# GpSimd issues two kinds of DMA of layer 0's experts: the loads of slots and the stores of results

## The chip, the cores and the metric

The kernel runs on one core of a Trainium2 chip. A core has five engines that run their own instruction streams and meet only at semaphores: TensorE (PE: matrix products; PEld is its weight load), VectorE (DVE), ScalarE (ACT), GpSimd (POOL) and SyncE (SP). DMAs are issued by an instruction in the stream of SP, ACT or GpSimd, and 16 DMA engines then move the data. An engine takes its instructions in order, so an instruction that waits holds up all that come after it on its engine.

The metric is the device time of one execution in microseconds. Before the change it is 2783.87 us, the median of three runs (2782.39 to 2789.58).

## The reference

The program is two layers on x of 8 x 512 tokens with 256 features, all float32. Layer 0 is what matters here:

```python
x = L0_attn_x
xn = _layernorm(x, axis=-1)
x = x + _L0_attn_ref(xn, ...) + _L0_ffn_ref(xn, L0_ffn_Wg, L0_ffn_W1, L0_ffn_W2, L0_ffn_W3)
xn = _layernorm(x, axis=-1)
x = x + _L1_attn_ref(xn, ...) + _L1_ffn_ref(xn, ...)
```

`_L0_attn_ref` is a linear recurrence in time, run forwards and backwards (16 heads, a state of 16 x 16 per head, a decay that depends on the token), with projections before it and a group norm and a projection after it. `_L0_ffn_ref` is a mixture of eight experts, of which each token takes the two with the highest scores:

```python
scores = xt @ Wg.T
topk_scores, topk_idx = jax.lax.top_k(scores, TOP_K)
gate = jax.nn.silu(jnp.einsum('td,ehd->teh', xt, W1))
up = jnp.einsum('td,ehd->teh', xt, W2)
y = jnp.einsum('teh,edh->ted', gate * up, W3)
out = jnp.einsum('te,ted->td', w, y)
```

Both parts of layer 0 read the same normed x, so they can be computed beside each other. Layer 1 is attention (one global, one local block) and another mixture of experts.

## The kernel before

**Routing and slots.** The kernel first norms and routes all eight sequences (`norm_and_route`, `place`). Each token and each of its two experts gets a slot, a row in the DRAM tensor `slots`; slots of one expert are together, in chunks of 256 rows. There are 39 chunks. `scatter` (L372) writes the tokens to their slots with 64 indirect DMAs on GpSimd.

**The experts.** `experts` (L410) goes through the chunks. For chunk i it has GpSimd gather the weights of the chunk's expert (`weights`, L386: `wgu` for gate and up, 1.4 MB in two buffers; `wdn` for down, 0.75 MB in one). `load_slots` (L394) loads the 256 rows of a chunk from `slots` into `xs` (two buffers), `turned` (L401) transposes them on TensorE, ACT copies the transposed rows to `xT` (L418), and TensorE computes gate and up in three parts (L426), ACT the silu (L452), VectorE the product (L435), and TensorE the down projection `y` (L465). ACT copies `y` to `ys` (L472, one buffer), and a DMA stores `ys` to the DRAM tensor `outs` (L473). The slots of chunk i + 1 are loaded while chunk i is computed, and transposed at the end of the products of chunk i. Layer 1 later gathers the rows of `outs` (L903).

**The recurrence.** `scans` (L674) goes through 128 steps: 8 sequences, 2 halves of the features, 8 pairs of values. A step multiplies a tile `kv` by k (L688), runs two scans forwards (L699) and two backwards (L703), multiplies by r (L708), all on VectorE, and leaves sums over the keys to TensorE (L714), which are issued for two steps at a time. The tile `kv` (four buffers) is filled one step ahead by `spread` (L660): eight DMAs of 64 KB on SP (L665), which read the projection v of that sequence from the DRAM tensor `vd`. `projections` (L480) computes the next sequence's v, k, r, decay and gates while the scans of one sequence run; it loads `xnT` on SP (L485), and GpSimd makes some of its additions (L572). `ending` (L726) norms and projects the result of a sequence (L737 to L785), with a product on GpSimd (L767), a load of x (L730) and a store (L785) on SP.

**What sets the order.** Layer 0 is written as generators. `scans` yields four times a step, and at each yield every running generator (the experts, the projections, the endings) goes on by one turn. The order in which these emit instructions is the order on TensorE, VectorE, ACT and SP: they are pinned by `manual_schedule` (L240, `PINNED` in L35). GpSimd is not pinned; a scheduler puts its instructions in order by its own estimate of when each can run. Waits are inserted automatically, from what each instruction reads and writes. DMAs signal their end on shared semaphores: those that SP and ACT issue take turns on eight of them, in the order of the program, and those that GpSimd issues on eight others; a DMA first waits until the one before it on its semaphore has ended.

Of the kernel before, what the change touches and what calls it, by code (L numbers as in the profile page):

```python
# [165 lines left out]
def two_layers(ctx: ExitStack, tc: tile.TileContext, a: dict, out: bass.AP):  # L166
    nc = tc.nc
    vec_e, act_e, pool_e, pe = nc.vector, nc.scalar, nc.gpsimd, nc.tensor
# [70 lines left out]
    with ExitStack() as l0:  # L239
# [146 lines left out]
        def weights(i, name, of, n, bufs):  # L386
            w = ew.tile([P, n], F32, tag=name, name=f"{name}_{i}", bufs=bufs)
            pool_e.indirect_dma_start(
                out=w, out_offset=None, in_=of,
                in_offset=bass.IndirectOffsetOnAxis(ap=wrow[:, i : i + 1], axis=0),  # L390
            )
            return w

        def load_slots(i):  # L394
            xs = ex.tile([P, NS, D], F32, tag="xs", name=f"xs_{i}", bufs=2)
            nc.sync.dma_start(
                xs, slots[i * CH : (i + 1) * CH].rearrange("(n p) d -> p n d", p=P)
            )
            return xs

        def turned(i, xs):  # L401
            ps = ps_gu.tile([P, NC, CH], F32, tag="gu", name=f"xsT_{i}")
            for c in range(NC):
                for n in range(NS):
                    pe.transpose(
                        ps[:, c, n * P : (n + 1) * P], xs[:, n, c * P : (c + 1) * P], ident
                    )
            return ps

        def experts():  # L410
            nxt = weights(0, "wgu", a["w0_gu"], GU0, 2)
            ps = turned(0, load_slots(0))
            yield
            for i in range(NCH):
                w, xps = nxt, ps
                wd = weights(i, "wdn", a["w0_dn"], DN0, 1)
                xT = ex.tile([P, NC, CH], F32, tag="xT", name=f"xsT_{i}", bufs=1)
                act_e.copy(xT, xps)  # L418
                if i + 1 < NCH:
                    nxt = weights(i + 1, "wgu", a["w0_gu"], GU0, 2)  # L420
                    xs = load_slots(i + 1)
                yield

                def hidden(o, at):
                    for c in range(NC):
                        pe.matmul(  # L426
                            o, w[:, at + c * P : at + (c + 1) * P], xT[:, c, :],
                            start=c == 0, stop=c == NC - 1,
                        )

                hs = [hpool.tile([P, 2, CH], F32, tag="h", name=f"h_{i}_{j}") for j in range(3)]

                def product(j, g, u):
                    n = 2 - j // 2
                    vec_e.tensor_tensor(hs[j][:, :n, :], hs[j][:, :n, :], u[:, :n, :], ALU.mult)  # L435
                    if n == 1:
                        o = hs[j][64:, 1, :]
                        vec_e.tensor_tensor(o, o, g[64:, 1, :], ALU.mult)

                last = None  # L440
                for j in range(3):
                    g = ps_gu.tile([P, 2, CH], F32, tag="gu", name=f"g_{i}_{j}")
                    hidden(g[:, 0, :], 4 * j * D)
                    hidden(g[:, 1, :], (4 * j + 2) * D)
                    yield
                    if last:
                        product(j - 1, *last)
                    u = ps_gu.tile([P, 2, CH], F32, tag="gu", name=f"u_{i}_{j}")
                    n = 2 - j // 2
                    for k in range(n):  # L450
                        hidden(u[:, k, :], (4 * j + 2 * k + 1) * D)
                    act_e.activation(hs[j][:, :n, :], g[:, :n, :], AF.Silu)  # L452
                    if n == 1:
                        act_e.activation(hs[j][64:, 1, :], g[:64, 1, :], AF.Silu)
                    last = g, u
                    yield
                if i + 1 < NCH:
                    ps = turned(i + 1, xs)
                product(2, *last)
                yield  # L460
                y = ps_gu.tile([P, NS, D], F32, tag="gu", name=f"y_{i}")
                for n in range(NS):
                    for j in range(NJ0 + 1):
                        lo = 64 * (j == NJ0)
                        pe.matmul(  # L465
                            y[:, n, :], hs[j // 2][lo:, j % 2, n * P : (n + 1) * P],
                            wd[lo:, j * D : (j + 1) * D], start=j == 0, stop=j == NJ0,
                        )
                        if j % 3 == 2:
                            yield  # L470
                ys = ex.tile([P, NS, D], F32, tag="ys", name=f"ys_{i}", bufs=1)
                act_e.copy(ys, y)  # L472
                act_e.dma_start(  # L473
                    outs[i * CH : (i + 1) * CH].rearrange("(n p) d -> p n d", p=P), ys
                )

# [326 lines left out]
        place()  # L803
        turns.finish()
        turns.add(then(scatter(), experts()))
        for _ in scans(turns):
            turns.turn()
# [616 lines left out]
```

## Time and profile before

| | |
|---|---|
| median of three runs | 2783.87 us |
| profiled execution, device time | 2787.46 us |
| its span, first to last instruction | 2785.7 us |
| PE, PEld busy | 2359.8 us (85%), 1402.9 us (50%) |
| DVE busy | 2137.6 us (77%) |
| ACT busy | 870.1 us (31%) |
| POOL busy | 407.2 us (15%) |
| first slot load, last scan of layer 0 | 237.4 us, 1476.5 us |

The profile is of one execution. Busy time is time in which an engine computes (or, on GpSimd, makes the descriptors of a DMA); instructions that only issue a DMA on SP or ACT are not counted, and stand under SPq and ACTq. "A <- B" in a list of waits means that A stood idle until B ended: total us, times, longest. A wait for several things is put down to the one that ended last, and a DMA's wait is named after the operation that moved the data, such as `kv<-vd`. The chain of waits follows the work that ended last from the end back to the start, at each step to what released it.

### The profile page before, as it was taken

The page shows a single profiled execution, that of the slowest core. Times are in us where ns is not written, and L with a number is a line of the kernel's source. Part 1 is how long each engine was busy: PE and PEld are TensorE (multiplying, and loading weights), DVE is VectorE, ACT ScalarE, POOL GpSimd, SP SyncE. Part 2 cuts the span into 40 slices and gives each one's busy share as a digit, 9 for nine tenths or more (in the row PEclk, how much of TensorE's full clock was granted, in tenths as well). Part 3 has the DMA queues.
Part 4 walks back from the last instruction along what each step waited for, and adds up shares of the span by engine and source line. Part 5 has one row for each costly group of instructions (what it writes and reads, how often), then busy time and mean ns, then how long its engine had stood idle before and what let it go on. Part 6 is the DMA issues. An engine that isn't in the chain of part 4 may idle for free.

```text
span 2785.7 us, 32431 instructions
## 1 busy us (share of the span) xinstructions
PE 2359.8 (85%) x11772; PEld 1402.9 (50%) x11772; DVE 2137.6 (77%) x3042; ACT 870.1 (31%) x1649; POOL 407.2 (15%) x368
## 2 busy tenths in 40 slices
PE   4756888988989889898873899999999989998996
PEld 3313555545555555555651445655555545555554
DVE  4698989899999899889894866667576676667656
ACT  1203231232312323122110234444333434343344
POOL 0074121221212112121102110001010100001000
PEclk8768998999999999999895899999998999999998
DMA  8245454445454444544543100010010100000000
GB/s 281 76 147 168 136 169 130 149 131 168 147 164 136 147 149 145 170 118 149 165 128 140 54 28 24 9 35 28 20 31 31 31 28 27 28 20 28 20 9 16
DMA packets 123886, 263.22 MB, mean 94 GB/s; under 512 B 25264, under 2 KB 76368, under 8 KB 118608
## 3 DMA queue, kind: packets, MB, share of 16 engines
q1 hardware_dynamic: 86912, 129.58, 16.4%
q0 software_dynamic: 17376, 103.69, 11.2%
q10 hardware_dynamic: 19440, 27.87, 2.7%
q8 instruction: 95, 1.56, 0.2%
q14 instruction: 63, 0.52, 0.1%
HBM read 215.17 MB, written 45.88 MB: 94 GB/s over the span
## 4 chain that ended last, share of the span: by engine, by line
PE 49%; DVE 26%; DMA 6%; ACT 4%; issue 3%; SPq 2%; POOL 1%; DVEq 0%; ACTq 0%; POOLq 0%
PE y L1307 6%; PE g L1261 5%; PE u L1261 5%; PE y L465 4%; DVE kv L699 4%; PE g L426 3%; DVE kv L703 3%; DMA kv<-vd 3%; PE sc_g L1159 2%; PE u L426 2%; PE o_g L1187 2%; PE ys L714 2%; SPq L665 2%; DVE kv L688 2%; PE qkv_l L1051 1%
## 5 line engine op out<-in xcount | busy, mean ns | idle before, releaser
L703 DVE TENSOR_TENSOR_SCAN kv<-d,kv 128x512 f32<-128x512 f32 x256 | 336.9, 1316 | 8.8
L699 DVE TENSOR_TENSOR_SCAN kv<-dq,kv 128x512 f32<-128x512 f32 x256 | 320.4, 1252 | 2.5
L426 PE MATMUL g<-xsT,wgu 128*128 128x256 f32 x936 | 249.3, 413 | 32.0 <-ACT xsT L418 31.9
L465 PE MATMUL y<-wdn,h 128*128 128x256 f32 x936 | 259.3, 416 | 11.9 <-DVE h L435 11.9
L1167 ACT ACTIVATE pt_g<-sc_g 128x512 f32<-128x512 f32 (+1 forms) x384 | 171.0, 531 | 237.4 <-PE sc_g L1159 202.8
L426 PEld LDWEIGHTS g<-xsT,wgu 128*128 128x128 f32 x936 | 188.3, 207 | 112.1 <-ACT xsT L418 51.4
L465 PEld LDWEIGHTS y<-wdn,h 128*128 128x128 f32 x936 | 173.8, 200 | 111.1 <-issue 76.7
L1261 PE MATMUL g<-xT,w 128*128 128x512 f32 x384 | 199.6, 645 | 24.4 <-DVE h L1296 9.4
L1261 PE MATMUL u<-xT,w 128*128 128x512 f32 x384 | 190.1, 618 | 18.7 <-DVE h L1296 7.6
L426 PE MATMUL u<-xsT,wgu 128*128 128x256 f32 x780 | 192.8, 387 | 0.0
L714 PE MATMUL ys<-kv,cst 128*32 128x512 f32 x512 | 122.1, 638 | 78.3 <-DVE kv L708 78.1
L688 DVE TENSOR_TENSOR kv<-kv,k 128x1024 f32<-128x1024 f32 x128 | 158.1, 1236 | 37.8 <-DMA kv<-vd 22.0
L1307 PE MATMUL y<-w,h 128*128 128x256 f32 x768 | 179.3, 385 | 0.0
L426 PEld LDWEIGHTS u<-xsT,wgu 128*128 128x128 f32 x780 | 151.6, 196 | 37.9 <-issue 14.8
L708 DVE TENSOR_TENSOR kv<-kv,r 128x1024 f32<-128x1024 f32 x128 | 160.8, 1257 | 3.7
L1279 DVE TENSOR_TENSOR h<-h,u 128x512 f32<-128x512 f32 x96 | 66.0, 688 | 120.5 <-PE u L1261 115.9
L1307 PEld LDWEIGHTS y<-w,h 128*128 128x128 f32 x768 | 141.7, 190 | 32.2 <-issue 9.5
L452 ACT ACTIVATE h<-g 128x512 f32<-128x512 f32 (+1 forms) x117 | 61.6, 526 | 287.8 <-PE g L426 280.2
L1173 DVE TENSOR_TENSOR pt_g<-pt_g,cst 128x512 f32<-128x512 f32 x128 | 85.2, 686 | 69.6 <-ACT pt_g L1167 69.5
L1261 PEld LDWEIGHTS g<-xT,w 128*128 128x128 f32 x384 | 72.5, 202 | 108.3 <-issue 83.9
L1167 ACT ACTIVATE pt_l<-sc_l 128x384 f32<-128x384 f32 (+1 forms) x256 | 98.0, 469 | 90.0 <-PE sc_l L1159 71.9
L1173 DVE TENSOR_TENSOR pt_l<-pt_l,cst 128x768 f32<-128x768 f32 (+1 forms) x128 | 107.9, 885 | 14.8 <-ACT pt_l L1167 14.8
(296 smaller groups left out, 3763.4 us busy)
## 6 DMA issues: line engine op xcount, KB each, us to landing
kv<-vd SPq DMA_DIRECT2D x1024, 64.0 KB, 2.7
cb<-cd SPq DMA_DIRECT2D x128, 128.0 KB, 2.9
slots<-zero SPq DMA_DIRECT2D x1, 9984.0 KB, 35.4
xs<-slots SPq DMA_DIRECT2D x39, 256.0 KB, 4.8
outs<-ys ACTq DMA_DIRECT2D x39, 256.0 KB, 2.1
w<-in_w ACTq DMA_DIRECT2D x12, 384.0 KB, 9.5
xn<-in_x SPq DMA_DIRECT2D x8, 512.0 KB, 8.7
xnT<-xT ACTq DMA_DIRECT2D x16, 256.0 KB, 2.1
```

What stands on the lines that cost most here:

```text
L426: pe.matmul(o, w[:, at + c * P : at + (c + 1) * P], xT[:, c, :], start=c == 0, stop=c == NC - 1,)
L465: pe.matmul(y[:, n, :], hs[j // 2][lo:, j % 2, n * P : (n + 1) * P], wd[lo:, j * D : (j + 1) * D], start=j == 0, stop=j == NJ0,)
L688: vec_e.tensor_tensor(kv, kv, bc(kc, 1, NV), ALU.mult)
L699: vec_e.tensor_tensor_scan(out=kv[:, i, :], data0=qc, data1=kv[:, i, :], initial=0.0, op0=ALU.mult, op1=ALU.add,)
L703: vec_e.tensor_tensor_scan(out=kv[:, i, ::-1], data0=dc[:, ::-1], data1=kv[:, i, ::-1], initial=0.0, op0=ALU.mult, op1=ALU.add,)
L708: vec_e.tensor_tensor(kv, kv, bc(rc, 1, NV), ALU.mult)
L714: pe.matmul(y[r0 : r0 + 32, :], C["take"][:, 24 - 8 * at : 56 - 8 * at], kv[:, i, :], start=at == 0, stop=at == 3, skip_group_check=True,)
L1167: act_e.activation(pt[:, i, :end], scs[i][:, :end], AF.Exp, scale=0.25)
L1173: vec_e.tensor_tensor(pt[:, :, a0 : a0 + m], pt[:, :, a0 : a0 + m], bc(mask[:, :m], 1, 4), ALU.mult,)
L1261: pe.matmul(ps, w[:, k, c * P : (c + 1) * P], xT[:, c, :], start=c == 0, stop=c == NC - 1,)
L1279: vec_e.tensor_tensor(hs[-1], hs[-1], u, ALU.mult)
L1307: pe.matmul(y[:, i, :], hs[k][:, (t + i) * P : (t + i + 1) * P], w1[j - 5 + k][:, 2, :], start=k == 0, stop=k == 5,)
```

## The change

Two DMA issues move to GpSimd's stream: `load_slots` is issued by GpSimd instead of SP (39 loads of 256 KB), and the store of `ys` by GpSimd instead of ACT (39 stores of 256 KB). The data, tiles and buffers stay as they are, and the order of the other instructions on TensorE, VectorE, ACT and SP too. GpSimd's own order is drawn up anew by the scheduler: the 78 DMAs stand among the gathers of weights, the additions of the projections and the products of the endings.

```diff
         def load_slots(i):
             xs = ex.tile([P, NS, D], F32, tag="xs", name=f"xs_{i}", bufs=2)
-            nc.sync.dma_start(
+            pool_e.dma_start(
                 xs, slots[i * CH : (i + 1) * CH].rearrange("(n p) d -> p n d", p=P)
             )
             return xs
...
                 ys = ex.tile([P, NS, D], F32, tag="ys", name=f"ys_{i}", bufs=1)
                 act_e.copy(ys, y)
-                act_e.dma_start(
+                pool_e.dma_start(
                     outs[i * CH : (i + 1) * CH].rearrange("(n p) d -> p n d", p=P), ys
                 )
```

## The prediction

> **What bounds the kernel now.** I read the busy shares first, then one stretch of layer 0, then the waits of VectorE and of SP's DMA queue in it, then the chain there. The change touches only the experts of layer 0, which run from 235 us (the first slots are loaded) to about 1480 us (the last scan). Busy time in that stretch (PE, PEld, DVE, ACT, POOL, each with its count; then TensorE's clock, DMA share, GB/s):
>
> ```profile
> 235.00:1480.00 1245.00, 1067.33 (x4078) 666.48 (x4078) 1129.97 (x1118) 312.07 (x483) 223.65 (x165) 0.93 0.49 147
> ```
>
> VectorE is busy 1130.0 of 1245 us (91%), TensorE 1067.3 (86%), GpSimd 223.7 (18%). So VectorE bounds the stage, with 115 us of idle time in it, and TensorE is close behind. What VectorE waited for (165 to 1500 us: total, times, longest):
>
> ```profile
> DVE kv L688 <- DMA kv<-vd: 22.0, 13, 5.0
> DVE x L782 <- PE o L777: 17.1, 10, 4.4
> DVE kv L688 <- DMA xs<-slots: 15.7, 5, 5.1
> ...
> DVE dx L514 <- DMA xnT<-xnT: 10.9, 2, 6.4
> ```
>
> Line 688 is the first operation of a scan step and needs that step's `kv`; it never reads `xs`. The 15.7 us are the same wait: a slot load stood in SP's queue with the `kv` loads and landed last. So 37.7 us of VectorE's idle time is late `kv`, and 10.9 us a late `xnT`, both loaded by SP. Why is SP late, with loads that could go a step ahead? SP's own waits, 235 to 1480 us:
>
> ```profile
> SPq L665 <- DMA outs<-ys: 389.2, 32, 26.0
> SPq L665 <- PE ys L714: 119.0, 26, 16.2
> SPq L396 <- DMA outs<-ys: 70.6, 7, 14.9
> SPq L665 <- DMA vd<-v: 48.6, 6, 12.1
> ```
>
> 39 waits, 459.8 us, end with the landing of a store of experts' results, which the `kv` load does not need. The instruction order of the built program tells why: the DMAs of SP and ACT share eight completion semaphores in turn, and a DMA first waits for the one that used its semaphore before. Each `outs` store takes a place in that rotation, so within eight DMAs SP stands still until the store has landed; that is after the chunk's product on TensorE and the copy on ACT. The chain of waits has it in full (start, us, what):
>
> ```profile
> 624.80 1.07 PE y L465 x4
> ...
> 625.90 0.59 ACT ys L472
> ...
> 626.51 2.08 DMA outs<-ys
> ...
> 628.62 0.30 SPq L665
> ...
> 628.96 3.50 DMA kv<-vd
> ...
> 632.58 1.24 DVE kv L688
> ```
>
> TensorE finishes `y`, the store takes 2.08 us, SP moves 0.02 us later, `kv` lands 3.50 us after its issue, and VectorE, idle for 2.23 us, starts. I looked at SP and the stores ahead of every VectorE wait over half a microsecond on `kv` (16): fourteen have this form; two (0.58 and 0.73 us) follow a `vd` store of the projections, which stays. Both `xnT` waits have it too.
>
> **What the skill says.** The Trainium skill, "DMA: Bandwidth & Descriptors", section "Issuing engines are not separate DMA queues": the 16 engines serve all issuers, so moving a DMA saves only issuing time. The trace shows more than that here: what SP loses is not 0.4 us of issue but a wait in its order. The same page, "SWDGE vs HWDGE vs iDMA": descriptors of GpSimd's DMAs are made in software, into rings in SBUF. "SBUF — State Buffer", "Who interferes with whom": a VectorE operation with two SBUF inputs contends with a GpSimd operation that reads SBUF. The trace agrees: scans of L703 last 1.22 us alone and 1.85 us on average beside GpSimd's additions of L572; beside its weight gathers (DMA_INDIRECT) they last 1.22, or 1.93 where an addition stood there too. I price the new issues' hold on VectorE at nothing.
>
> **The change, part by part.** Sums are against the profiled execution (2787.46 us, span 2785.7); that is 3.6 us above the median of the three runs, 2783.87, and I take the same difference off the median.
>
> ```profile
> xs<-slots SPq DMA_DIRECT2D x39, 256.0 KB, 4.8
> outs<-ys ACTq DMA_DIRECT2D x39, 256.0 KB, 2.1
> ...
> wgu<-in_w_gu,wrow POOLq DMA_INDIRECT x39, 7.8
> wdn<-in_w_dn,wrow POOLq DMA_INDIRECT x39, 6.2
> ```
>
> *Removed from SP.* 39 issues of 0.42 us (16 us of SP time, off the path), and with both kinds gone from the rotation, its waits on `outs`. What then holds a `kv` load is its buffer (four; it was last read by TensorE's sums of four steps earlier, which TensorE does some two steps of about 10 us ahead) and its predecessor in the rotation, the `kv` load just before. Eight issues of 0.42 us and 2.7 us of landing are 6 us, within a step. So 37.7 - 1.3 + 10.9 = 47.3 us of VectorE's stalls go. How much stays gained is a choice: VectorE, released, meets TensorE sooner (`x` behind `o`, 17.1 us), but TensorE itself waits 78.1 us for VectorE's L708 and gets that earlier. Between half and all, I take three quarters: -35.5.
>
> *Removed from ACT.* The store's issue (0.37 us) stands between the copy of `ys` and that of `xsT`, 0.44 us in all, for which TensorE waits at 24 chunk starts (1.7 us each): 24 x 0.44 = 10.6 us of TensorE's time. It is not the bound; I take a quarter: -2.6.
>
> *Added to GpSimd.* 78 issues. No row shows a direct DMA issued there; the nearest, the weight gathers, take 0.94 to 1.98 us, mean 1.3. 78 x 1.3 = 101 us, so its busy time goes from 224 to 325 of 1245 us. What counts is who stands behind. In GpSimd's new order a slot load follows the gather of `wgu` for the chunk before its own and waits for the transposes that free its buffer; a store follows the gather of `wdn` and waits for ACT's copy, which by then has ended but for 0.3 us at most, the last chunk apart. Replaying the new order on the old times (1.3 us per issue, dependencies where they were), 23 slot loads stand over 1 us (47 us in all), mostly before a gather that waits anyway; of the 60 additions of L572 four groups are late by 1.3 to 2.2 us (7.0 in sum) and three of the products of L767 by 1.3 (4.0). TensorE uses them two turns later, about 5 us minus the additions themselves; I charge a quarter, +3.
>
> *The DMAs themselves.* The bytes are the same. In GpSimd's queue a load stands behind up to 1.4 MB of weights: landing may go from 4.8 to some 16 us (`wgu` 12.8 at most, and 3), but it is wanted almost two chunks later, over 40 us. A store lands perhaps 10 us after its issue instead of 2.1; the one buffer of `ys` is written again a chunk later, 22.3 us at the least. That cover is gone above 22 us: then ACT, and TensorE behind it, wait.
>
> *At the start.* `xs` of chunk 0 went out at 237.41, when the last scatter landed, and was there at 240.1; TensorE waited 14.5 us, VectorE 8.3. Now it stands behind the gather of `wdn` on GpSimd (236.28 to 238.23) and in the queue behind its 0.75 MB, landing 1.8 to 5 us later: +3.5.
>
> Sum: -35.5 - 2.6 + 3 + 3.5 = -31.6. 2787.46 becomes 2755.9, and 2783.87 becomes **2752**.
>
> **Rivals.** (1) *Both engines profit.* If TensorE too runs ahead, half of VectorE's other waits over 0.5 us (46 us: on TensorE, ACT) go as well: 47.3 + 23 - 4 = 66, 2718. For it: L708's 78.1 us on TensorE. Against: TensorE is 86% busy already. (2) *The stall moves to TensorE.* VectorE arrives earlier and waits for `o`, for projections, or a `kv` buffer that TensorE frees late (119.0 us of SP's waits end with the sums of L714). A quarter of the gain stays: 12 - 4 = 8, 2776. The end of it is that nothing changes: the loads stay as late as before for another reason, 2784. (3) *Slower: GpSimd's issue.* If a direct DMA of 256 rows costs GpSimd much more than a gather of 128, additions and products pile up behind it. In the same replay, 4 us per issue makes L572 and L767 late by 98 us over single instructions, about half that by groups of those that follow each other; at 6 us it is 180, some 90 by groups. If TensorE pays all of it, against 35 us of gain without this term, 6 us means +55, 2839, and it decides above roughly 3 us an issue. Against it: the scatters, also 128 rows of 1 KB, take 0.97 us, so 256 should stay below 2.6.
>
> **How the numbers follow.** Main case, half to all of 47.3 us: 0.6, its own range 2740 to 2765. Rival 1: 0.1. Rival 2: 0.2, of which 0.1 between -0.3% and the main case's edge and 0.1 at no change. Rival 3: 0.1. The range runs from 2722, inside rival 1, to 2782, through rival 2. Measurements of this kernel tell 0.3% (8 us) from no change: faster 0.8, same 0.1, slower 0.1.
>
> **What would show it.** SP's waits on `outs` gone and VectorE's on `kv` below 10 us; the new issues on GpSimd at 1 to 2.6 us; TensorE's waits on L572 (5.6 us) below 15; its wait for the first `xs` longer, about 18 us. I am wrong if L688 still waits for `kv` by 30 us, if waits on TensorE grow by what those lose, or if layer 1, after 1500 us, changes its length by more than 5 us.

## The result, and the profile after

The changed kernel takes 2754.25 us (median of 6 runs, 2747.16 to 2761.39) against 2785.2 us before (6 runs on the same chip, 2779.6 to 2790.13): ratio 0.9889, 95% interval 0.9868 to 0.9909, so 31 us faster. The forecast was 2752.

The profiled execution of the changed kernel has a span of 2745.4 us, 40.3 less than before. It is the fastest of its six runs, and the profile before lies 2.3 us above its median, so the two profiles differ by more than the medians do. I cut both spans at the same two marks, the last scatter and the end of the last product with r (L708). Of the 40.3 us, 2.3 lie ahead of the experts, 1.85 in the last ending, 3.25 in layer 1 (1285.85 to 1282.6 us), and 32.9 in the stretch that the change touches. Busy time there by stretch, before and after (columns as in the prediction: stretch and its length, PE, PEld, DVE, ACT, POOL, clock, DMA share, GB/s):

```profile
235.00:1478.90 1243.90, 1066.31 (x4074) 666.29 (x4074) 1129.93 (x1118) 312.07 (x483) 223.65 (x165) 0.93 0.49 147
```

and after:

```profile
232.70:1443.70 1211.00, 1054.13 (x4074) 660.18 (x4074) 1134.46 (x1118) 308.14 (x483) 289.52 (x243) 0.93 0.50 150
```

VectorE's idle time fell from 1243.90 - 1129.93 = 114.0 to 1211.00 - 1134.46 = 76.5 us, by 37.5; its busy time rose by 4.5. The 78 additional instructions on GpSimd (165 to 243) are the moved issues. GpSimd's busy time rose by 65.9 us; the issues are 57.8 of that, and its gathers of `wdn` took 6.2 us more. What SP waited for in the stretch, after the change (235 to 1445 us; total, times, longest):

```profile
SPq L665 <- PE ys L714: 417.7, 56, 24.1
SPq L665 <- DVE kv L708: 90.1, 30, 11.3
SPq L665 <- DMA vd<-v: 78.6, 6, 15.5
```

The 459.8 us on `outs` are gone. SP still waits as long, but now chiefly for a free `kv` buffer (the sums of L714), and `kv` is there when VectorE needs it, as the next list shows. VectorE's waits after (165 to 1470 us):

```profile
DVE xf L568 <- PE m L563: 14.6, 2, 11.4
DVE x L782 <- PE o L777: 13.8, 9, 4.4
DVE dq L640 <- ACT near L636: 11.6, 7, 2.2
DVE q L626 <- ACT d L621: 8.8, 6, 2.1
```

No wait on `kv` and none on `xnT` is left anywhere in the list; before they stood first, third and further down, with 48.6 us. The longest wait is now the one of 11.4 us at the start, 8.3 us before. The moved issues on GpSimd (line, operation, count; busy us, mean ns; idle before them and what ended it), and then their landing times from the page's list of DMA issues:

```profile
L473 POOL DMA_DIRECT2D outs<-ys x39 | 29.1, 745 | 22.0 <-ACT ys L472 20.6 <-issue 1.4
L396 POOL DMA_DIRECT2D xs<-slots x39 | 28.7, 736 | 45.3 <-PE xsT L405 45.3
```

```profile
xs<-slots POOLq DMA_DIRECT2D x39, 256.0 KB, 7.2
outs<-ys POOLq DMA_DIRECT2D x39, 256.0 KB, 5.7
```

An issue costs GpSimd 0.74 us, 57.8 us in all. GpSimd stands 45.3 us before slot loads, waiting for the transposes that free `xs`. A load lands 7.2 us after its issue instead of 4.8, a store 5.7 instead of 2.1.

### The profile page after: what moved, and what is told of

Read it like the earlier page. It is cut to its first block, busy times and chain, and to the rows that moved or that the text cites. A ratio compares the mean times of both kernels' runs of the same rounds, so it can differ in the third digit from the quotient of the medians.

```text
span 2745.4 us, 32489 instructions
## 1 busy us (share of the span) xinstructions
PE 2338.7 (85%) x11772; PEld 1392.8 (51%) x11772; DVE 2141.9 (78%) x3042; ACT 865.9 (32%) x1649; POOL 472.3 (17%) x446
## 3 DMA queue, kind: packets, MB, share of 16 engines
q8 instruction: 95, 1.56, 0.2%
## 5 line engine op out<-in xcount | busy, mean ns | idle before, releaser
L699 DVE TENSOR_TENSOR_SCAN kv<-dq,kv 128x512 f32<-128x512 f32 x256 | 324.8, 1269 | 2.5
L426 PE MATMUL g<-xsT,wgu 128*128 128x256 f32 x936 | 248.0, 412 | 20.1 <-ACT xsT L418 19.6
L714 PE MATMUL ys<-kv,cst 128*32 128x512 f32 x512 | 123.2, 653 | 79.0 <-DVE kv L708 78.8
L708 DVE TENSOR_TENSOR kv<-kv,r 128x1024 f32<-128x1024 f32 x128 | 160.2, 1251 | 3.7
L688 DVE TENSOR_TENSOR kv<-kv,k 128x1024 f32<-128x1024 f32 x128 | 160.2, 1251 | 0.0
L903 POOL DMA_INDIRECT y<-outs,slot x64 | 64.7, 1010 | 324.8 <-DVE acc L911 312.6
```

What stands on the lines that cost most here:

```text
L426: pe.matmul(o, w[:, at + c * P : at + (c + 1) * P], xT[:, c, :], start=c == 0, stop=c == NC - 1,)
L688: vec_e.tensor_tensor(kv, kv, bc(kc, 1, NV), ALU.mult)
L699: vec_e.tensor_tensor_scan(out=kv[:, i, :], data0=qc, data1=kv[:, i, :], initial=0.0, op0=ALU.mult, op1=ALU.add,)
L708: vec_e.tensor_tensor(kv, kv, bc(rc, 1, NV), ALU.mult)
L714: pe.matmul(y[r0 : r0 + 32, :], C["take"][:, 24 - 8 * at : 56 - 8 * at], kv[:, i, :], start=at == 0, stop=at == 3, skip_group_check=True,)
```

## The experiments

Theory: the gain comes from the stores, which no longer take a place among the DMAs of SP and ACT, so that `kv` and `xnT` are in time for VectorE. The rivals were ACT's time, the slot loads, GpSimd's issue cost, and TensorE taking the gain back. Each comparison is with runs of the kernel before on the same chip; those medians lay between 2785 and 2798 us. The two highest, 2796.11 and 2797.81, stand beside the kernels with `kv` two steps ahead and the 1 KB store on GpSimd; the ratio of the latter is lower for that reason alone. The granted TensorE clock does not account for the gain: it is 0.93 in the stretch before and after, and beside the repeat of the changed kernel (2753.55 to 2763.01 us at 0.921 to 0.924) the runs of the kernel before at 0.92 and above took 2778.14 to 2786.5 us.

| kernel | median us | ratio to before, 95% interval |
|---|---|---|
| changed kernel | 2754.25 | 0.9889 (0.9868 to 0.9909) |
| the same again | 2754.65 | 0.9892 (0.9870 to 0.9914) |
| stores alone moved | 2756.12 | 0.9887 (0.9872 to 0.9902) |
| loads alone moved | 2790.96 | 1.0014 (1.0000 to 1.0028) |
| changed, 1 KB store on ACT | 2808.91 | 1.0079 (1.0066 to 1.0092) |
| changed, 1 KB store on GpSimd | 2754.30 | 0.9833 (0.9794 to 0.9871) |
| changed, ACT busy instead | 2759.45 | 0.9901 (0.9887 to 0.9916) |
| changed, DMAs in four pieces | 2758.69 | 0.9910 (0.9887 to 0.9932) |
| changed, first transposes late | 2755.60 | 0.9890 (0.9866 to 0.9914) |
| stores alone, first transposes late | 2770.60 | 0.9940 (0.9919 to 0.9962) |
| before, kv two steps ahead | 2820.06 | 1.0096 (1.0066 to 1.0125) |
| changed, kv two steps ahead | 2759.09 | 0.9881 (0.9841 to 0.9920) |

None of these kernels leaves a part of the computation out. The 1 KB stores and the additional copy write data that nothing reads.

### One half of the change at a time

Stores alone:

```diff
-                act_e.dma_start(
+                pool_e.dma_start(
                     outs[i * CH : (i + 1) * CH].rearrange("(n p) d -> p n d", p=P), ys
                 )
```

> Only the stores move to GpSimd; the slot loads stay on SP. Theory (the stores' places in the semaphore rotation of SP and ACT made SP wait for the end of each chunk): all of the gain is here, SP's waits on outs (460 us) are gone and VectorE's L688 waits for kv under 8 us; the first slots come as early as before, so about 3 us better than the full change: 36 us below before, ratio 0.987. Rival (the slot loads in SP's queue, ahead of the kv loads, were the hindrance: 15.7 us of L688's waits ended with one): L688 still waits 15 us or more, at most 20 us below before, ratio 0.993 or above.

Loads alone:

```diff
-            nc.sync.dma_start(
+            pool_e.dma_start(
                 xs, slots[i * CH : (i + 1) * CH].rearrange("(n p) d -> p n d", p=P)
             )
```

> Only the slot loads move to GpSimd; the stores stay on ACT. Theory: SP still waits for outs over 400 us in total and L688 still waits for kv some 30 us (each stall shorter by the 0.42 us of a slot load's issue at most, 16 x 0.42 = 7 us); the start is 3 us later; in all within 8 us of before, ratio 0.997 to 1.002. Rival (slot loads in SP's queue): 15 to 25 us below before, ratio 0.991 to 0.995.

Measured: 2756.12 us with the stores alone, 2790.96 with the loads alone. The stores carry the whole gain, which is 31 us with them alone, as with the full change, and not 5 more; the loads bring nothing. SP's longest waits with the loads alone (200 to 1480 us), and VectorE's on what SP loads (165 to 1460 us):

```profile
SPq L665 <- DMA outs<-ys: 455.5, 39, 26.9
SPq L665 <- PE ys L714: 168.5, 28, 24.0
```

```profile
DVE kv L688 <- DMA kv<-vd: 39.8, 21, 5.2
...
DVE dx L514 <- DMA xnT<-xnT: 10.6, 2, 5.6
```

39 waits on `outs`, as many as there are chunks, and 50.4 us of VectorE's stalls, as before the change. The 15.7 us that stood under `xs<-slots` before stand under `kv<-vd` here (37.7 then, 39.8 now): that a slot load landed last in those waits did not make it their cause. With the stores alone VectorE has no wait on `kv`. Its stretch is 1212.60 us long, against 1211.00 and 1216.30 in the two profiles of the full change.

### A store of 1 KB, on ACT and on GpSimd

To separate the place in the rotation from the transfer, the changed kernel got one more small store after each chunk's store, once on ACT and, as its control, once on GpSimd:

```diff
+        mark = dram.tile([NCH, D], F32, name="mark", bufs=1)
...
+                act_e.dma_start(mark[i : i + 1, :], ys[0:1, 0, :])
```

> The changed kernel, with one more DMA per chunk: ACT, after its copy to ys, writes one row of it (1 KB) to a scratch tensor that nothing reads. The stores and slot loads stay on GpSimd. So a place in the rotation of SP and ACT is taken again, at the same point, with 1 KB instead of 256 KB. Theory: SP waits for this write as it did for outs (over 350 us), L688 waits 30 us or more, and the gain is given back: ratio to before 0.997 to 1.003. Rivals (the gain came from the bytes, from SP's shorter queue, or from ACT): only ACT's issue of 0.37 us is back, 3 us above the changed kernel, ratio 0.990.

> The control of the kernel with the 1 KB mark on ACT (2808.9 us): the same mark after each chunk's store, issued by GpSimd instead of ACT, so that it takes a place among GpSimd's DMAs and none among those of SP and ACT. Theory (the place in the rotation costs): SP waits on no mark, VectorE on no kv, and the time is that of the changed kernel plus at most 39 issues of 0.6 us on GpSimd, of which little counts: 2752 to 2764. Rival (an additional DMA after each chunk, or a second reader of ys, costs by itself whoever issues it): above 2780.

On ACT 39 KB in all undo more than the whole gain: 2808.91 us. On GpSimd the same stores cost nothing that can be measured: 2754.30. SP's longest waits with the mark on ACT (200 to 1480 us), and VectorE's first (165 to 1480 us):

```profile
SPq L667 <- DMA mark<-ys: 424.0, 39, 26.0
```

```profile
DVE kv L690 <- DMA kv<-vd: 38.1, 21, 4.3
```

With the mark on GpSimd, SP's longest waits (200 to 1480 us) and the group of the marks' issues on GpSimd:

```profile
SPq L667 <- PE ys L716: 405.5, 57, 15.3
```

```profile
L477 POOL DMA_DIRECT2D mark<-ys x39 | 20.9, 537 | 0.0
```

SP stands before `kv` buffers again, as in the changed kernel, and a mark costs GpSimd 0.54 us. Neither the bytes nor a second reader of `ys` matters, but whose order the DMA stands in. This shows the cause: a DMA on ACT that waits for a chunk's result holds up SP's loads. Moving a DMA to GpSimd changes more than its semaphores, but the trace names these: in the kernel before, the DMA that comes next on the semaphore of a store, for each of the 39, is one of SP that waits on it; for 31 of them it is also the first DMA that SP issues after the store's landing, 0.02 us later. In the changed kernel no SP DMA waits on the semaphore of a store.

The mark on ACT makes the kernel slower than before, by 0.8%. In its profile, which is of the fastest of its five runs (2797.71 us), the stretch is 1258.80 us, 14.9 longer than before: VectorE is busy 7.7 us more and idle 7.2 more, of which 3 is the later start. The full change brings costs of the same kind (4.5 us of busy time, 3.1 at the start), so with its gain lost about half of the 14.9 us was to be expected. The rest, and why the other four runs are slower by 6.6 to 12.4 us, stays open.

### ACT's time

A copy of 128 x 128 after that of `ys` puts ACT's time back without a DMA:

```diff
                 act_e.copy(ys, y)
+                act_e.copy(ex.tile([P, P], F32, tag="pad", name=f"pad_{i}", bufs=1), ys[:, 0, :P])
```

> The changed kernel, with an ACT copy of 128x128 from ys to a tile that nothing reads, between the copies of ys and xsT of every chunk: ACT's 0.37 us come back as work, without a DMA. Theory: a quarter of what TensorE waits for it counts, 2 to 3 us above the changed kernel (ratio to before 0.990). Rival (TensorE is the bound after the change, so its 24 to 39 waits of 0.3 to 0.4 us count in full): 8 to 15 us above it, ratio 0.992 to 0.995.

TensorE's wait for ACT's copy of `xsT` went back from 19.6 us (18 times, longest 1.2) to 27.6 (24 times, longest 1.5), where before the change it was 31.9 (24 times, longest 1.7). The median is 5.2 us above the changed kernel's, but the stretch (1216.00 us) lies within the two profiles of the changed kernel, and the intervals overlap. By the stretches ACT's part is 0 to 5 us of the 31; the ratios differ by 3 us, with an uncertainty of about 7 (an estimate from the two intervals). The copy put back 8.0 of the 12.3 us of TensorE's wait.

### GpSimd's issue cost

Each slot load and each store is cut into four DMAs of 128 rows by 512 B, all on GpSimd:

```diff
-            pool_e.dma_start(
-                xs, slots[i * CH : (i + 1) * CH].rearrange("(n p) d -> p n d", p=P)
-            )
+            for n in range(NS):
+                for h in range(2):
+                    pool_e.dma_start(
+                        xs[:, n, h * P : (h + 1) * P],
+                        slots[i * CH + n * P : i * CH + (n + 1) * P, h * P : (h + 1) * P],
+                    )
...
-                pool_e.dma_start(
-                    outs[i * CH : (i + 1) * CH].rearrange("(n p) d -> p n d", p=P), ys
-                )
+                for n in range(NS):
+                    for h in range(2):
+                        pool_e.dma_start(
+                            outs[i * CH + n * P : i * CH + (n + 1) * P, h * P : (h + 1) * P],
+                            ys[:, n, h * P : (h + 1) * P],
+                        )
```

> The changed kernel, with each slot load and each store of results cut into four DMAs (128 rows of 512 bytes each), all on GpSimd: 312 issues instead of 78. At the 0.73 us that an issue took, a load or a store now holds GpSimd for about 3 us. Theory (GpSimd has room; what is late there is mostly paid by VectorE in a few longer scans): 5 to 15 us above the changed kernel, ratio to before 0.991 to 0.995. Rival 3 of the prediction (from 3 us on, the late additions and products of GpSimd eat the gain): no faster than before, ratio 0.998 or more, TensorE waiting over 30 us for L572's additions.

The pieces on GpSimd, by group:

```profile
L398 POOL DMA_DIRECT2D xs<-slots x156 | 85.6, 558 | 43.8 <-PE xsT L408 39.2 <-issue 2.6 <-DMA wgu<-in_w_gu,wrow 1.9
L478 POOL DMA_DIRECT2D outs<-ys x156 | 84.9, 551 | 23.3 <-ACT ys L475 21.0 <-issue 2.2
```

Four pieces come to 2.2 us for a load or a store, less than I had assumed and three times what one issue costs, and 170.5 us on GpSimd instead of 57.8. The time is 2758.69 us, some 4 above the changed kernel run beside it, with overlapping intervals. In its profile the stretch is 1215.20 us, with VectorE busy for 1143.09, 8.6 more than in the changed kernel. So tripling the issue cost takes a few us, if anything: at 0.74 us an issue it is far from deciding.

### The start

The changed kernel's first slot load stands behind a gather. If TensorE does not stand before the first transposes but goes on with the projections, that should not matter. The edit, to the changed kernel and to the one with the stores alone:

```diff
-            ps = turned(0, load_slots(0))
+            xs = load_slots(0)
+            for _ in range(6):
+                yield
+            ps = turned(0, xs)
             yield
```

> The changed kernel, with the transposes of the first chunk put into TensorE's order six turns later (the load is issued as before), so that TensorE goes on with the projections while the first slots arrive. Theory: its wait for the first slots (17.7 us) and VectorE's stall behind it (11.4 us) go, 8 to 12 us below the changed kernel, ratio to before 0.985. Rival (the experts, some 15 us later, end after the scans and lengthen the end of layer 0 by as much): within 3 us of the changed kernel.

> The changed kernel itself, on the same chip as the others of this call: ratio 0.989, so that differences between it and the others are taken without a change of chip.

> Only the stores on GpSimd (slot loads on SP), with the first chunk's transposes six turns later as in the other kernel. Theory: the loads' engine does not matter, so the same as that one, ratio 0.985, within 4 us of it; the first slots, issued by SP without the weights ahead of them, are no longer waited for either. Rival (the loads on SP cost when SP runs ahead): 5 us or more above it.

The start did what the edit says: TensorE's wait for the first `xs` fell from 17.7 to 5.7 us and VectorE's 11.4 us are gone. Nothing of that reached the end: 2755.60 us, and 2754.65 for the changed kernel beside it. VectorE's longest waits from 235 us on, with the late transposes:

```profile
DVE x L785 <- PE o L780: 14.9, 8, 3.6
DVE xf L571 <- PE m L564: 14.6, 6, 6.7
```

Its idle time in the stretch is 76.0 us, and 76.5 and 80.7 in the two profiles of the changed kernel: what was saved at the start went into other waits on TensorE, those on `o` (7.4 us after the change in the same list, 14.9 here) and on the `m` of L561, L564 here (6.3 and 14.6). The time is as the rival had it, but not for its reason: the last store went out later, at 1439.9 us instead of 1421.2, but still before the last scans.

With the stores alone the edit makes things worse: 2770.60 us, 14.5 above the stores alone and 15.0 above the changed kernel with the same edit. My theory had within 4 us of the latter; the rival, that loads on SP cost when SP runs ahead, had 5 or more. Its waits of VectorE (235 to 1470 us) show part of it:

```profile
DVE q L629 <- ACT d L624: 11.4, 3, 5.5
DVE kv L691 <- DMA kv<-vd: 6.2, 2, 3.2
DVE z L768 <- PE rs L766: 6.1, 3, 2.6
```

In the changed kernel with the same edit these are 4.1, none and 0.9 us; here VectorE's idle time is 94.0 us instead of 76.0. So with the slot loads left on SP a `kv` can still be late; why in this order and not in that of the stores alone stays open.

### Loading kv earlier instead

If the stores hurt only because `kv` is late, could the kernel before load `kv` two steps ahead and leave GpSimd alone? There are four buffers.

```diff
-                if n + 1 < len(todo) and (todo[n + 1][0] in made):
-                    kvs[todo[n + 1]] = spread(*todo[n + 1])
+                for t in todo[n + 1 : n + 3]:
+                    if t not in kvs and t[0] in made:
+                        kvs[t] = spread(*t)
```

> The kernel before, GpSimd left alone: SP loads the slots and ACT stores the results, but each kv is loaded two steps ahead instead of one (its four buffers allow it). Theory (the stores cost time only because they make kv late for VectorE): SP goes on waiting some 300 to 450 us on outs, yet VectorE's waits on kv, 37.7 us before, fall below 8; the 10.9 us on xnT stay. With the four fifths that the changed kernel kept of its removed stalls that is 30 us: 2753 to 2762. Rival (a store on ACT costs by itself, through ACT's issue or through TensorE, and the late kv is only a sign of it): above 2772, although kv is in time. Rival (SP loses two steps as easily as one): VectorE's waits on kv stay above 25, and the time above 2775.

> The changed kernel with each kv loaded two steps ahead. Theory: kv is no longer late in the changed kernel, so there is nothing to gain: 2750 to 2760, no wait of VectorE on kv. Rival (the wait of SP for kv buffers that TensorE frees late, 418 us, still costs something through the projections' loads, which stand behind the kv loads in SP's order): SP now stands before a buffer earlier in the order, xnT and the endings' loads are later, and the time is above 2763. If it is below 2748, the lead of kv was still short somewhere that the waits do not name.

My theory's number fell, and clearly: 2820.06 us, 1% slower than before. The second rival held. SP's waits on `outs` (235 to 1500 us) and VectorE's on SP's loads (165 to 1520 us) in the kernel before with two steps:

```profile
SPq L665 <- DMA outs<-ys: 399.2, 35, 26.9
...
SPq L731 <- DMA outs<-ys: 39.3, 2, 19.6
```

```profile
DVE dx L514 <- DMA xnT<-xnT: 37.3, 4, 11.5
DVE kv L688 <- DMA kv<-vd: 25.9, 13, 5.5
```

SP waits on `outs` as long as before (438.5 us, then 459.8). VectorE's stalls on `kv` fall only from 37.7 to 25.9, and those on `xnT`, whose load got no longer lead, rise from 10.9 to 37.3: 63.2 us in all, 14.6 more than before. TensorE then waits for the `dx` made of that `xnT` (44.1 us, before 17.9). The stretch is 1280.70 us, 36.8 longer than before, with VectorE busy 7.1 more and idle 29.7 more. I read it so, without a run that isolates it: a longer lead lets VectorE run on until the next load that has none. In the changed kernel, where no store stands in the way, the same edit costs little or nothing: 2759.09 us. There VectorE waits for no `kv`, but for `xnT` twice again (8.4 us, none without the edit), so the edit by itself makes `xnT` later.

## Why the prediction was right

**The cause held.** The step that put 459.8 us of SP's waits, and through them VectorE's on `kv` and `xnT`, down to the stores' places in the rotation is shown by three runs: with the stores alone moved all of it goes, with the loads alone none, and a store of 1 KB on ACT brings it back (424.0 us of SP, 38.1 of VectorE on `kv`), but not on GpSimd. The Trainium skill, "DMA: Bandwidth & Descriptors", section "Issuing engines are not separate DMA queues", says that spreading DMAs over issuing engines saves only issuing time; here moving the stores saved 31 us, of which ACT's time is a small part, and the measurement decides: what went was a wait of SP.

**The sizes**, against the stretch's -32.9 us (forecast -31.6):

| step | forecast us | measured us |
|---|---|---|
| stalls on kv, xnT that go | 47.3 | 48.6 |
| kept of them, with ACT's part | -35.5 - 2.6 = -38.1 | -40.6 |
| late additions on GpSimd | +3 | +4.5 |
| start | +3.5 | +3.1 |
| sum | -31.6 | -33.0 |

The -40.6 is VectorE's idle time without the start, -37.5 - 3.1, and the +4.5 is its busy time; the two and the start add up to the stretch by construction, so only the single terms test the forecast. The -40.6 cannot be parted by profile between SP and ACT. The two stalls behind a `vd` store, said to stay with 1.3 us, went too.

The second profile of the same kernel, of a run at its median, has a stretch of 1216.30 us, which would make it -27.6, with -36.5 for what is kept. So terms of 3 us are near what two profiles differ by, and that they agree so closely is partly luck. The medians give 31.0.

**Kept of the stalls.** Three quarters was a choice between half and all; 40.6 of 48.6 is 84%, and 36.5 in the second profile 75%, both with ACT's help. TensorE's wait for VectorE's L708 did not shrink as I had argued (78.1, then 78.8 us); what shrank were its waits for ACT's `xsT` (31.9 to 19.6) and for `dx` (17.9 to 9.6).

**ACT.** TensorE's wait for `xsT` fell by 12.3 us where I had 10.6. (1.7 us was the longest of its 24 waits, not each; they are 31.9 us in all, 1.3 on average. The sum does not use it.) That a quarter of it counts lies within what the run with ACT busy allows.

**GpSimd's issue: the step that was mis-sized.** I took 1.3 us from the nearest row, the gathers, with 0.94 to 2.6 as bounds; it is 0.74, below the lower one. A gather of 128 rows was no measure for a direct DMA of 256. The landing times were overestimated too: at most 10.3 us for a load (estimate 16), at most 7.9 for a store (estimate 10), so the cover of 22.3 us before `ys` is written again was never near its end. Rival 3, which needed 3 us an issue, therefore had no chance; at 2.2 us, in pieces, the medians differ by 4 us, with overlapping intervals.

**Who pays for late additions: TensorE, and VectorE as well.** The delays are about as many as the replay had: five groups of additions and four products start right behind an issue, and the replay had four and three late. But I had TensorE alone pay, and put what the late additions cost VectorE at nothing. TensorE's waits on L572 went from 5.6 to 9.5 us. VectorE paid too: its busy time is up 4.5 us, 4.4 of them in the scans of L699 (298.4 to 302.8). One place in the timeline, before and then after (start, us, engine, line):

```profile
527.69 6.22 POOL L572 TENSOR_TENSOR xf<-xf,xnT 128x512 f32<-128x512 f32 x4
...
529.25 1.80 DVE L699 TENSOR_TENSOR_SCAN kv<-dq,kv 128x512 f32<-128x512 f32 x1
531.09 1.93 DVE L703 TENSOR_TENSOR_SCAN kv<-d,kv 128x512 f32<-128x512 f32 x1
```

```profile
517.65 0.73 POOL L473 DMA_DIRECT2D outs<-ys  x1
...
518.41 4.23 POOL L572 TENSOR_TENSOR xf<-xf,xnT 128x512 f32<-128x512 f32 x4
519.18 4.54 DVE L699 TENSOR_TENSOR_SCAN kv<-dq,kv 128x512 f32<-128x512 f32 x1
```

Before, four additions and the scans beside them stretched each other: 6.22 us for the additions, some 0.6 to 0.7 for each scan. After, the additions start behind the store's issue, only 0.77 us ahead of a scan; they take their plain 4.23 us, and that one scan lasts 4.54 and ends at 523.72, behind the last of them (522.64). Four scans of L699 last over 2.5 us in the changed kernel (4.54 and three of 2.8), each with a store's issue just ahead and then these additions, or a product of L767, on GpSimd; before, no scan lasts over 2.3. Against 1.22 us alone, these four are 8.1 us longer, of which the sharing that went gives some back. That the two engines contend agrees with the Trainium skill, "SBUF — State Buffer", section "Who interferes with whom", which the prediction used for the issues themselves and not for what they delay; a hold through four additions is this trace's own.

**The start** was right as a local size (VectorE 8.3 to 11.4, TensorE 14.5 to 17.7 us) and wrong as a term of the end: taken away, it gave nothing back, and without it (stores alone) the kernel is no faster.

**The rivals.** Rival 1 (TensorE runs ahead too) did not come: VectorE's waits on TensorE did not halve. Rival 2 came in a small part: of 48.6 us some 8 went into other waits, chiefly on TensorE, such as `xf` behind L561 (2.1 to 6.3 us) and `h` behind `u` (2.5 to 5.1). Layer 1 stayed within the 5 us.

## What to carry to other kernels

Where DMAs of several engines take turns on a few semaphores, a store that waits for late data holds up the loads that come after it in program order, whatever its size; look in the issuing queue's waits for the landing of a transfer that the waiting load does not need. The cure here was to put the late store into another order. Loading `kv` earlier did not help: it stayed late in part, and the next load without a lead, `xnT`, came later still. When work is moved to an engine with time to spare, price what it delays there, and also what the delayed work then stands beside.

## What the hardware showed that I had not expected

- A direct DMA of 256 rows of 1 KB holds GpSimd for 0.74 us, one of 128 rows of 512 B for 0.55, one row of 1 KB for 0.54. So most of it does not depend on the size; the gathers of 128 rows took 1.33 and 1.44 us on average after the change.
- These issues do not slow VectorE: 64 scans and 21 of the products of L688 and L708 that overlapped one in the changed kernel, and no addition or product of GpSimd, took 1.22 us on average, as they do alone.
- Scans on VectorE and additions on GpSimd met in two forms: sharing (1.80 and 1.93 us for a scan, 1.56 for an addition) and one scan held through all the four additions beside it (4.54 us). In both profiles of the changed kernel and in that of the stores alone, the scans held by four additions began 0.77 to 0.82 us behind the first of them, and those held by a product of L767 (2.75 to 2.83 us) began 0.38 to 0.46 us ahead of it. What decides between the two forms was not tried.
